# Causal mask and row maximum of a diagonal score tile in one VectorE instruction, in a planned transformer block

## The chip, the cores and the metric

The kernel runs on one core of one Trainium2 chip. The core has TensorE (PE, matmuls into PSUM banks; PEld are its weight loads), VectorE (DVE), ScalarE (ACT), GpSimd (POOL) and SyncE (SP, which issues most DMAs). Each engine works through its own instruction queue in order, and semaphores hold an instruction until what it needs is done. The metric is device time in microseconds of one execution. Before the change the median of three runs is 1046.6 us (1046.23 to 1047.99); the profiled execution took 1046.28 us, of which the span from the first to the last instruction is 1044.4 us.

## The reference

A macaron block over x of shape (4, 1024, 256), all in fp32: half a feed-forward layer, causal attention with 16 heads of 16 features, half a feed-forward layer again.

```python
x = x + 0.5 * ffn(layernorm(x))
x = x + attn(layernorm(x))
x = x + 0.5 * ffn(layernorm(x))

# attn: q, k with rotary embedding
att = einsum('bhqd,bhkd->bhqk', q, k) / sqrt(hd)
mask = triu(full((T, T), -inf), k=1)
att = softmax(att + mask, axis=-1)
out = einsum('bhqk,bhkd->bhqd', att, v)

# ffn: INTER = 704
hdn = silu((x @ gate_w.T) * gate_s) * ((x @ up_w.T) * up_s)
out = (hdn @ down_w.T) * down_s
```

## The kernel before

The 4096 rows are eight blocks of 512 tokens (two to a sequence of 1024). A block goes through feed-forward 1 (`ffn`), the projections (`qkv`), attention and feed-forward 2; several blocks are under way at once so that dense matmuls fill TensorE while attention waits for the vector engines. Matmuls come in two modes. Column matmuls (feed-forward, projections, probabilities times values) use four groups of 32 array columns side by side; row matmuls (scores) use four groups of 32 array rows, one head each. All dense products are recorded under L470, score matmuls under L859 (for the maxima) and L972 (for the exponentials), probabilities times values under L1019.

Attention makes the scores twice. `max_half` computes scores with queries on partitions for two heads of a group of four and takes the row maximum on VectorE; `row_of_max` turns the maxima (L939, a matmul with the identity), copies them to SBUF (L942) and sends them by DMA (L947) into a spare row of the queries, so that `exp_half`, which makes the scores again with keys on partitions, has the maximum subtracted by the matmul itself. ScalarE then takes the exponential from PSUM (L981), GpSimd zeroes what lies above the diagonal (L993), and `weigh` multiplies with the values. A max half and an exp half of different head pairs run at the same time as one burst on four row groups; each half owns two PSUM banks, one for each head `e` of its pair, until its last reader is done. One or two bursts in a row make a visit to row mode.

The units of `max_half` for one block and a pair of groups `gs`: off the diagonal (second block of a sequence only) whole tiles of 512 keys; on the diagonal, for each of the two groups, one of 512 and one split into 384 + 128, and one shared by both groups, 256 + 256. A unit's entry is (group, query tile, key block, first column, width, masked). On a diagonal entry the last 128 columns cross the diagonal. There, before the change, an addition of the 128x128 tile `causal` (zero and -1e30) masks these columns in PSUM (L884), and a reduction with `negate=True` takes the negative maximum into a column of the tile `nm` (L911, or L894 with one instruction for both groups of the shared unit). Where a sequence has two key blocks, L933 joins the two parts with a minimum.

Nothing of the order is left to a compiler's scheduler. The class `Planner` keeps a modelled time for each engine, with a duration and a priority for each `Op` (`dve_us(n)` is n/960 + 0.07), and places next whatever can start first, or a burst (`step`). PSUM has eight banks, shared between bursts ("score") and dense outputs ("d", at most four). A few thresholds (`GAP`, `LONG`, `SECOND`, `DUE`, `OPEN`) say how long bursts are held back; `draw` sets them anew after each eight bursts, from a table of seeds, which before the change is empty (all thresholds at their defaults). So a changed duration of one step moves instructions on all engines.

Of the kernel before, what the change touches and what calls it, by code (L numbers as in the profile page):

```python
# [13 lines left out]
F32 = mybir.dt.float32  # L14
AF = mybir.ActivationFunctionType
ALU = mybir.AluOpType
AX = mybir.AxisListType
PSUM = bass.MemoryType.PSUM

P = 128  # L20
EPS = 1e-5
MASKED = -1e30
DRAWS = ()


class Buf:
# [20 lines left out]
class Planner:  # L47
# [3 lines left out]
    ENGINES = ("pe", "dve", "act", "pool", "dma")  # L51
    GAP = 0.8
    LONG = 7.0
    VISIT = 2
    SECOND = 0.3
    OPEN = 3.0
# [111 lines left out]
    def step(self, burst):  # L168
        b = burst()

        more = self.mode == "row" and self.visit < self.VISIT and b is not None and {h.kind for h in b[1]} != {"max"}
        due = b is not None and (more or self.since >= self.GAP)
        best = None
        for eng in self.ENGINES:
            for c in self.candidates(eng):
                s = max(c[0], self.busy["pe"] + 0.05) if eng == "pe" else c[0]
                if eng == "pe" and due and any(k.slot is None and k.kind == "d" for k in c[2].takes):
                    s += self.DUE
                key = (s, c[1] + (self.luck[eng] * self.random() if self.luck[eng] else 0.0))
                if best is None or key < best[0]:  # L180
                    best = (key, c)
        if b is not None:
            pe = self.busy["pe"]
            at = max(b[0], pe)
            if more:
                wait = self.SECOND
            else:
                wait = self.WAIT[self.mode]
                if self.since < self.GAP:
                    at += self.GAP - self.since  # L190
                elif self.since < self.LONG and b[2] is not None:
                    at = max(at, b[2] - 0.853 - 0.2 - self.SECOND)
            key = (max(at, pe + 0.05) - wait, 0)
            if best is None or key < best[0]:
                halves = b[1]
                us = max(h.us for h in halves) + 0.02 + (0.0 if self.mode == "row" else self.CHANGE["row"])
                if self.mode == "row":

                    us += min(max(b[0] - pe + 0.2, 0.0), 0.1)
                at = max(b[0], pe, at if self.since >= self.GAP else 0.0)  # L200
                for h in halves:
                    h.us = us
                    self.place(h, at)
                self.visit = self.visit + 1 if self.mode == "row" else 1
                self.mode, self.since = "row", 0.0
                self.bursts += 1
                self.draw()
                return b
        assert best is not None, "nothing can be placed"
        (s, _), (at, _, op, q) = best  # L210
        if op.eng == "pe":
            self.since += op.us
            if op.mode != self.mode:
                op.us += self.CHANGE[op.mode]
                self.mode = op.mode
        self.place(op, at)
        for o in op.then:
            self.since += o.us
            self.place(o, self.busy["pe"])
        if q is not None:  # L220
            q.popleft()
        else:
            self.loose[op.eng].remove(op)
            self.unplaced -= 1
        return None
# [6 lines left out]
def dve_us(n):  # L232
    return n / 960 + 0.07
# [7 lines left out]
def tile_macaron(  # L241
# [16 lines left out]
    nc = tc.nc  # L258
# [51 lines left out]
    wo_sb = cpool.tile([P, NC, D], F32, name="wo_sb")  # L310
    rope_sb = cpool.tile([P, 2, T], F32, name="rope_sb")
    ident = cpool.tile([P, P], F32, name="ident")
    causal = cpool.tile([P, P], F32, name="causal")
    mhalf = cpool.tile([P, 2], F32, name="mhalf")
    lasting = dict(
        kT=[cpool.tile([P, NG, BLK], F32, name=f"kT_{i}", tag=f"kT_{i}") for i in range(3)],
# [28 lines left out]
    def consts():  # L345
        nc.scalar.dma_start(out=gus_sb, in_=gus)
        nc.scalar.dma_start(out=ds_sb, in_=ds.partition_broadcast(P))
        nc.scalar.dma_start(out=wd_sb[HALF:, NF, :], in_=wl)
        at = 0
        for a, e in cuts:  # L350
            part = wgu[at : at + D * (e - a)].rearrange("(p c i) -> p c i", p=P, c=NC)
            nc.sync.dma_start(out=wgu_sb[:, :, a:e], in_=part)
            at += D * (e - a)
        nc.sync.dma_start(out=wd_sb[:, :NF, :], in_=wd)
        nc.gpsimd.memset(mhalf, -0.5)
        make_identity(nc, ident)
        make_causal_mask(nc, causal, mask_val=MASKED)

    def scaled_gus():

# [483 lines left out]
    def row_at(g, part, h, j):  # L844

        return g % 2 * HP + part * GH * NB + h * NB + j

    def max_half(blk, unit, pair, nm, reduces):

        parts = 1 + blk % BPS  # L850
        sc = [Buf("score") for _ in range(2)]
        tiles = [kT[blk - parts + 1 + u[2]] for u in unit]

        def emit():

            for (g, j, _, c0, w, _), kt in reversed(list(zip(unit, tiles))):
                for e in range(2):
                    r = slice((2 * pair + e) * HP, (2 * pair + e) * HP + HD)
                    nc.tensor.matmul(  # L859
                        sc[e].tile[:, c0 : c0 + w],  # L860
                        qT[blk].tile[r, g, ts(j, P)],
                        kt.tile[r, g, :w],
                        start=True,
                        stop=True,
                    )

        gs = {u[0] // 2 for u in unit}
        need = [T_done[1, b, n] for b in range(blk - blk % BPS, blk + 1) for n in gs]
        first = Op(
            "pe", mm_us(sum(u[4] for u in unit)), emit, need, [*sc, nm], [qT[blk], *tiles], mode="row", tail=0.25  # L870
        )
        masked = [(c0 + w - P, c0 + w) for _, _, _, c0, w, m in unit if m]

        def head(e):
            prev = first
            if masked:

                def mask():
                    a, z = masked[0][0], masked[-1][1]
                    if masked[0][1] == masked[-1][0] or len(masked) == 1:  # L880
                        d = sc[e].tile[:, a:z].rearrange("p (m k) -> p m k", k=P)
                    else:
                        d = sc[e].tile.rearrange("p (m k) -> p m k", k=2 * P)[:, :, P:]
                    nc.vector.tensor_tensor(d, d, causal.unsqueeze(1).to_broadcast([P, len(masked), P]), ALU.add)  # L884

                prev = Op("dve", dve_us(P * len(masked)), mask, [first], uses=[sc[e]], prio=0, tail=0.1)
                loose_att.append(prev)

            if unit[0][0] != unit[-1][0]:
                j, part = unit[0][1:3]  # L890

                def reduce():
                    o = row_at(0, part, 2 * pair + e, j)
                    nc.vector.tensor_reduce(  # L894
                        nm.tile[:, o : o + HP + 1 : HP],
                        sc[e].tile.rearrange("p (g k) -> p g k", g=2),
                        AX.X,
                        ALU.max,
                        negate=True,
                    )  # L900

                o = Op("dve", dve_us(BLK), reduce, [prev, *filled["nm"]], uses=[sc[e], nm], prio=0, tail=0.25)
                loose_att.append(o)
                for g in (unit[0][0], unit[-1][0]):
                    reduces[g].append(o)
            else:
                for g, j, part, c0, w, _ in unit:

                    def reduce(g=g, j=j, part=part, c0=c0, w=w):
                        o = row_at(g, part, 2 * pair + e, j)  # L910
                        nc.vector.tensor_reduce(  # L911
                            nm.tile[:, o : o + 1], sc[e].tile[:, c0 : c0 + w], AX.X, ALU.max, negate=True
                        )

                    o = Op("dve", dve_us(w), reduce, [prev, *filled["nm"]], uses=[sc[e], nm], prio=0, tail=0.25)
                    loose_att.append(o)
                    reduces[g].append(o)

        for e in range(2):
            head(e)  # L920
        first.pair, first.kind = pair, "max"
        return first

    def row_of_max(blk, g, nm, reduces):
# [3 lines left out]
        if blk % BPS:  # L928

            def both():  # L930
                o = [row_at(g, n, 0, 0) for n in range(2)]
                a, b = (nm.tile[:, n : n + GH * NB] for n in o)
                nc.vector.tensor_tensor(a, a, b, ALU.min)  # L933

            need = [Op("dve", 0.09, both, reduces, uses=[nm], prio=0)]
            loose_att.extend(need)
# [2 lines left out]
            nc.tensor.matmul(d.tile[:HP, :P], nm.tile[:, ts(g % 2, HP)], ident, start=True, stop=True)  # L939

        def copy():
            nc.scalar.copy(t.tile, d.tile[: GH * NB, :P])  # L942

        def send(pair):
            for h in (2 * pair, 2 * pair + 1):
# [359 lines left out]
```

## Time and profile before

| | before |
|---|---|
| median of 3 runs | 1046.6 us |
| profiled execution | 1046.28 us |
| its span | 1044.4 us |
| granted TensorE clock | 1.000 |
| VectorE busy at L884 (masks), 320 instructions | 103.9 us |
| VectorE busy at L911 (reduces), 640 instructions | 330.3 us |
| VectorE busy at L894 (reduces for two groups), 64 instructions | 40.8 us |
| VectorE busy in all | 808.5 us |

Busy time counts an engine's instructions that move or compute data, overlapping ones once. The means in the groups are those of single instructions and hold the overlap with the next. The page's digit rows divide the span into 40 slices and give tenths; PEclk is at 9 (90% or more) in all of them. The chain of waits follows the work back from the last instruction, at each step to what released it. Matmul ends are modelled, so that PE is shown busy also where it loses time between matmuls; its starts are measured.

### The profile page before, as it was taken

Reading aid. Unit: us, or ns where it says so; the run is one execution under the profiler, and the core shown is the slowest. Engines: PE = TensorE matmul, PEld = TensorE weight load, DVE = VectorE, ACT = ScalarE, POOL = GpSimd, SP = SyncE. Lnnn points to the kernel's source line nnn. Section 1 sums busy time; section 2 is a strip of 40 time slices with the busy share of each in tenths; the row PEclk is TensorE's granted clock in tenths of the full one; section 3 lists DMA queues with packets and bytes.
Section 4 is the critical chain, followed back from the end, with each engine's and each line's share of the span. In section 5 each row is a group of like instructions: output and inputs, shape, how many; then the busy total and the mean of one; then the engine's idle time right before and its main releaser. Section 6 shows DMA issues by size and latency. Waiting matters only on the chain.

```text
span 1044.4 us, 28697 instructions
## 1 busy us (share of the span) xinstructions
PE 1036.3 (99%) x12162; PEld 442.7 (42%) x12162; DVE 808.5 (77%) x1876; ACT 429.7 (41%) x821; POOL 295.1 (28%) x501
## 2 busy tenths in 40 slices
PE   9999999999999999999999999999999999999998
PEld 5434443343444444443434443342434443434443
DVE  6679889788898887888897798778896797884432
ACT  3314341444453452435454434544354444455411
POOL 5222542231121633312115424221226211112200
PEclk9999999999999999999999999999999999999999
DMA  7211202102020021111010103101012010010000
GB/s 290 62 42 38 66 3 62 42 2 62 22 42 23 12 61 34 37 48 22 32 52 8 37 2 72 32 13 52 3 38 50 22 39 22 12 52 3 21 22 22
DMA packets 37969, 41.10 MB, mean 39 GB/s; under 512 B 3985, under 2 KB 27729, under 8 KB 37713
## 3 DMA queue, kind: packets, MB, share of 16 engines
q1 hardware_dynamic: 37184, 38.81, 14.1%
q8 instruction: 95, 1.56, 0.6%
q10 hardware_dynamic: 656, 0.47, 0.2%
q14 instruction: 34, 0.27, 0.1%
HBM read 19.60 MB, written 15.20 MB: 33 GB/s over the span
## 4 chain that ended last, share of the span: by engine, by line
PE 92%; DVE 6%; DMA 1%; issue 0%; ACT 0%; SPq 0%; DVEq 0%
PE bank L470 54%; PE bank L859 17%; PE bank L1019 12%; PE bank L972 10%; DVE nm L911 1%; DVE bank L884 1%; DVE xs L491 1%; DVE nm L894 1%; PE bank L939 0%; DVE hT L626 0%; DVE ta L623 0%; DMA xd<-xs 0%; PE bank L520 0%; DVE ta L603 0%; DVE hL L606 0%
## 5 line engine op out<-in xcount | busy, mean ns | idle before, releaser
L981 ACT ACTIVATE pT<-bank 128x512 f32<-128x512 f32 x576 | 298.5, 603 | 307.5 <-PE bank L972 306.7
L911 DVE TENSOR_REDUCE nm<-bank 128x1 f32<-128x512 f32 (+2 forms) x640 | 330.3, 573 | 20.0 <-PE bank L972 17.8
L470 PE MATMUL bank<-xnT,wgu_sb 128*32 128x512 f32 (+1 forms) x2832 | 321.5, 592 | 0.3
L859 PE MATMUL bank<-kT,qT 16*128 16x512 f32 (+3 forms) x1536 | 286.8, 511 | 2.2 <-DVE x L1104 0.9
L972 PE MATMUL bank<-qT,kT 17*128 17x512 f32 (+3 forms) x1536 | 286.7, 514 | 0.0
L470 PEld LDWEIGHTS bank<-xnT,wgu_sb 128*32 128x32 f32 x2832 | 92.0, 109 | 194.6 <-issue 122.1
L993 POOL TENSOR_SCALAR_AFFINE_SELECT pT<-pT 128x256 f32<-128x256 f32 x256 | 99.1, 407 | 263.9 <-ACT pT L981 263.0
L859 PEld LDWEIGHTS bank<-kT,qT 16*128 16x128 f32 x1536 | 111.3, 184 | 141.7 <-issue 35.3
L470 PE MATMUL bank<-wd_sb,hT 128*32 128x256 f32 x2560 | 152.4, 379 | 0.0
L1019 PE MATMUL bank<-pT,va 128*32 128x512 f32 (+3 forms) x1536 | 137.5, 487 | 0.4 <-DVE nm L911 0.2
L884 DVE TENSOR_TENSOR bank<-bank,causal 128x256 f32<-128x256 f32 (+1 forms) x320 | 103.9, 370 | 20.3 <-PE bank L972 15.1
L972 PEld LDWEIGHTS bank<-qT,kT 17*128 17x128 f32 x1536 | 109.4, 184 | 9.4 <-issue 2.6
L470 PEld LDWEIGHTS bank<-wd_sb,hT 128*32 128x32 f32 x2560 | 85.4, 110 | 55.1 <-issue 2.6
L620 ACT ACTIVATE ta<-bank,gus_sb 128x512 f32<-128x512 f32 x80 | 55.0, 687 | 113.2 <-PE bank L470 100.8
L623 DVE SCALAR_TENSOR_TENSOR ta<-ta,bank 128x512 f32<-128x512 f32 x80 | 54.6, 683 | 44.4 <-ACT ta L620 43.6
L1019 PEld LDWEIGHTS bank<-pT,va 128*32 128x32 f32 x1536 | 51.7, 109 | 83.5 <-issue 59.9
L1058 POOL TENSOR_TENSOR oq<-oq 128x512 f32<-128x512 f32 x32 | 40.7, 1273 | 154.8 <-DVE oq L1055 151.9
L1055 DVE STREAM_TRANSPOSE oq<-bank 128x512 f32<-128x512 f32 x64 | 45.5, 711 | 35.1 <-PE bank L1019 34.5
L626 DVE SCALAR_TENSOR_TENSOR hT<-bank,gus_sb,ta 128x512 f32<-128x512 f32 x80 | 59.5, 744 | 16.7 <-PE bank L470 15.5
L652 DVE TENSOR_TENSOR x<-bank,x 128x256 f32<-128x256 f32 x64 | 26.8, 418 | 49.7 <-PE bank L470 49.3
L731 POOL TENSOR_TENSOR qs<-qs,rope_sb 128x512 f32<-128x512 f32 x32 | 40.8, 1277 | 79.7 <-DVE qs L728 60.0
L470 PE MATMUL bank<-xnT,wqkv_sb 128*32 128x512 f32 x512 | 60.6, 595 | 0.1
(61 smaller groups left out, 649.0 us busy)
## 6 DMA issues: line engine op xcount, KB each, us to landing
xd<-xs SPq DMA_DIRECT2D x84, 128.0 KB
xnT<-xd SPq DMA_DIRECT2D x21, 512.0 KB
kT<-qT SPq DMA_DIRECT2D x64, 64.0 KB
x<-in_x SPq DMA_DIRECT2D x7, 512.0 KB
out<-x SPq DMA_DIRECT2D x14, 256.0 KB
qT<-nmT SPq DMA_DIRECT2D x128, 2.0 KB
wgu_sb<-in_wgu SPq DMA_DIRECT2D x2, 512.0 KB
rope_sb<-in_rope SPq DMA_DIRECT2D x1, 1024.0 KB
```

Of the source, the lines that this page charges most:

```text
L470: nc.tensor.matmul(out[ts(m, HP)], w[:, ts(m, HP)], x, **kw)
L620: nc.scalar.activation(a.tile, d.tile, AF.Tanh, scale=gus_sb[:, 0, c : c + 1])
L623: nc.vector.scalar_tensor_tensor(a.tile, a.tile, 1.0, d.tile, ALU.add, ALU.mult)
L626: nc.vector.scalar_tensor_tensor(hT[c].tile, e.tile, gus_sb[:, 1, c : c + 1], a.tile, ALU.mult, ALU.mult)
L859: nc.tensor.matmul(sc[e].tile[:, c0 : c0 + w], qT[blk].tile[r, g, ts(j, P)], kt.tile[r, g, :w], start=True, stop=True,)
L884: nc.vector.tensor_tensor(d, d, causal.unsqueeze(1).to_broadcast([P, len(masked), P]), ALU.add)
L911: nc.vector.tensor_reduce(nm.tile[:, o : o + 1], sc[e].tile[:, c0 : c0 + w], AX.X, ALU.max, negate=True)
L972: nc.tensor.matmul(sc[e].tile[:, c0 : c0 + w], kt.tile[r, g, ts(k % NB, P)], qT[blk].tile[r, g, BLK - w :], start=True, stop=True,)
L981: nc.scalar.activation(pT.tile[:, e, :w], sc[e].tile[:, :w], AF.Exp)
L993: nc.gpsimd.affine_select(out=d, in_=d, compare_op=ALU.is_ge, fill=0.0, base=0, pattern=[[0, 2], [1, P]], channel_multiplier=-1,)
L1019: nc.tensor.matmul(av.tile[ts(r, HP), BLK - w :], va[base + k // NB].tile[:, k % NB, h * VS : h * VS + HP], pTs[u, r // 2].tile[:, r % 2, ...
L1055: nc.vector.transpose(o.tile, av.tile)
```

## The change

Masking and reducing a diagonal entry become one VectorE operation, `tensor_tensor_reduce`: it adds `causal` to the scores, writes the sum back to the bank, and keeps the running maximum, which goes to the column of `nm`. As it runs over the entry's whole width, `causal` grows to 128x512, zero in the first 384 columns, and each entry uses its last `w` columns. The shared unit gets two such operations in place of one reduction for both groups. The operation can't negate its maximum, so maxima stay positive until L942, where the copy becomes a multiplication by -1, and L933 takes a maximum. In the planner, a fused step has the duration `dve_us(w)`. A new rule (`SLACK`) holds a step of lower priority back on VectorE and ScalarE when an urgent one becomes ready while it would run, unless it would end within 0.3 us (VectorE) or 0.1 us (ScalarE) of that. The table `DRAWS` gets 36 seeds, one for each eight bursts: 0 means the defaults, a negative seed moves each threshold by up to 3%, a positive one draws them from wide ranges and adds a random part to priorities.

```diff
-DRAWS = ()
+DRAWS = (
+    0, 607770, -440924, -671785, 0, 0, 0, 0, 518923, 731658, 0, 0, 0, 342111, -717196, -551854,
+    520586, 932614, 0, 0, -22380, 0, 556666, 0, 883259, 627517, 102005, 0, -129261, -32818, 0,
+    0, -79134, 466540, -412283, 867698,
+)
...
+    SLACK = dict(dve=0.3, act=0.1)
...
-            for c in self.candidates(eng):
+            found = list(self.candidates(eng))
+            first = min((c[0] for c in found if c[1] == 0), default=None) if eng in ("dve", "act") else None
+            for c in found:
                 s = max(c[0], self.busy["pe"] + 0.05) if eng == "pe" else c[0]
...
+                if first is not None and c[1] and s < first < s + c[2].us - self.SLACK[eng]:
+
+                    s = first + 0.001
...
-    causal = cpool.tile([P, P], F32, name="causal")
+    causal = cpool.tile([P, BLK], F32, name="causal")
...
-        make_causal_mask(nc, causal, mask_val=MASKED)
+        nc.gpsimd.memset(causal[:, : BLK - P], 0.0)
+        make_causal_mask(nc, causal[:, BLK - P :], mask_val=MASKED)
...
-                    nc.vector.tensor_tensor(d, d, causal.unsqueeze(1).to_broadcast([P, len(masked), P]), ALU.add)
-
-                prev = Op("dve", dve_us(P * len(masked)), mask, [first], uses=[sc[e]], prio=0, tail=0.1)
-                loose_att.append(prev)
-
-            if unit[0][0] != unit[-1][0]:
+            if unit[0][0] != unit[-1][0] and not any(u[5] for u in unit):
...
+            for g, j, part, c0, w, m in unit:
+
+                def reduce(g=g, j=j, part=part, c0=c0, w=w, m=m):
+                    o = row_at(g, part, 2 * pair + e, j)
+                    a, n = sc[e].tile[:, c0 : c0 + w], nm.tile[:, o : o + 1]
+                    if m:
+
+                        nc.vector.tensor_tensor_reduce(a, a, causal[:, BLK - w :], 1.0, MASKED, ALU.add, ALU.max, n)
+                    else:
+                        nc.vector.tensor_reduce(n, a, AX.X, ALU.max)
+
+                o = Op("dve", dve_us(w), reduce, [first, *filled["nm"]], uses=[sc[e], nm], prio=0, tail=0.25)
+                loose_att.append(o)
+                reduces[g].append(o)
...
-                nc.vector.tensor_tensor(a, a, b, ALU.min)
+                nc.vector.tensor_tensor(a, a, b, ALU.max)
...
-            nc.scalar.copy(t.tile, d.tile[: GH * NB, :P])
+            nc.scalar.mul(t.tile, d.tile[: GH * NB, :P], -1.0)
```

## The prediction

> **What bounds the kernel now.** I read the page first (busy time and the chain of waits), then a table by stretches of the span, then groups by form for VectorE's prices, and last the timeline around two attention bursts.
>
> ```profile
> span 1044.4 us, 28697 instructions
> PE 1036.3 (99%) x12162; PEld 442.7 (42%) x12162; DVE 808.5 (77%) x1876; ACT 429.7 (41%) x821; POOL 295.1 (28%) x501
> ...
> DVE  6679889788898887888897798778896797884432
> ...
> PE 92%; DVE 6%; DMA 1%; issue 0%; ACT 0%; SPq 0%; DVEq 0%
> ```
>
> ```profile
> 60.00:950.00 890.00, 887.13 (x10336) 374.42 (x10332) 740.81 (x1719) 386.77 (x744) 255.82 (x438) 1.00 0.14 34
> ```
>
> The columns of the second fence are the stretch, its length, then PE, PEld, DVE, ACT, POOL busy and the granted clock (1.00). The reader is to see two things: TensorE fills the span, and VectorE, which the change relieves, fills 740.8/890 = 83% of the stretch in which attention runs. A busy PE is not a PE at its peak, so I cut the PE timeline wherever row matmuls (scores, L859 and L972) and column matmuls (the rest) change places, and compare each piece with its columns.
>
> ```profile
> 417.56 0.42 PE bank L972 x2
> 417.98 0.01 PE bank L859 x2
> 417.99 1.91 PE bank L470 x32
> 419.89 0.63 PE bank L859 x2
> ...
> 421.83 1.86 PE bank L470 x32
> ```
>
> These are pieces of the chain: start, length, work. Four matmuls of 512 columns run side by side in 0.853 us where nothing interrupts (weight loads of a long L470 stretch come in fours every 0.43 us, two passes each), which is 2,400 columns per us over all four. The column piece at 417.99 holds two such groups, 1.71 us, and takes 1.91; the row visit at 419.89 holds two bursts, again 1.71, and takes 1.94.
>
> Over the whole trace: 2,265,088 columns / 2,400 = 943.8 us of work that no order can shorten. On top, 160 column pieces each lose at least 0.16 us (median 0.17: 26.4 us in all), 133 two-burst visits lose 0.25 to 0.36 us by shape and 22 one-burst visits 0.22 (together some 45 us). This is the price of changing mode. What is left over these floors is only **15 us of real stalls**, 5 in row visits and 10 in column pieces; in most of the largest (0.9 us at 170, 0.6 at 783, 0.6 at 235) the row's first weight load waited for a VectorE operation (L1104, L626, L1055). About 14 us lie at the two ends and in the transposes. So a VectorE saving can win at most 15 us, whatever its size.
>
> **The change, part by part.** *Mask and reduce become one step.* Prices before:
>
> ```profile
> L911 DVE TENSOR_REDUCE nm<-bank 128x1 f32<-128x512 f32 x384 | 240.5, 680 | 20.0 <-PE bank L972 17.8 <-PE bank L859 1.7
> L884 DVE TENSOR_TENSOR bank<-bank,causal 128x256 f32<-128x256 f32 x192 | 72.5, 423 | 11.5 <-PE bank L972 9.6 <-ACT va L769 1.5 <-PE bank L859 0.3
> ...
> L623 DVE SCALAR_TENSOR_TENSOR ta<-ta,bank 128x512 f32<-128x512 f32 x80 | 54.6, 683 | 44.4 <-ACT ta L620 43.6
> ...
> L933 DVE TENSOR_TENSOR nm<-nm 128x16 f32<-128x16 f32 x16 | 2.6, 163 | 0.0
> ...
> L728 DVE LOAD_MASK_SELECT qs<-bank x32 | 0.4, 13 | 12.3 <-PE bank L470 8.4 <-POOL qT L734 3.1 <-POOL on L1074 0.7
> ```
>
> The columns after the bar are busy us and mean ns of one. A mean contains the overlap with the next, so I take the step from start to start:
>
> ```profile
> 430.17 0.49 DVE L884 TENSOR_TENSOR bank<-bank,causal 128x128 f32<-128x128 f32 x2
> 430.56 1.27 DVE L911 TENSOR_REDUCE nm<-bank 128x1 f32<-128x512 f32 x2
> ...
> 434.12 0.76 DVE L884 TENSOR_TENSOR bank<-bank,causal 128x256 f32<-128x256 f32 x2 [0.31 <-PE bank L972]
> 434.80 1.41 DVE L911 TENSOR_REDUCE nm<-bank 128x1 f32<-128x384 f32 x4
> ```
>
> Two 128-wide masks 0.39, so 0.198 each; two 256-wide 0.68, so 0.33 each; reduces step by 0.598 (512), 0.465 (384) and 0.198 (128). Mask and reduce follow one line, width/960 us + 0.065. For each block, pair of groups, pair and head of the pair (8 x 2 x 2 x 2 = 64 times) there are two diagonal 512 units, two 384+128 units, and one 256+256 unit. Before: 2 x (0.198 + 0.598) + 2 x (0.331 + 0.465 + 0.198) + (0.331 + 0.598) = 4.51 us, times 64 = 288.6 us. The built order of the changed kernel has 512 fused steps and, behind each, a second VectorE instruction that writes one column of nm. At the same line the fused steps take 2 x 0.598 + 2 x (0.465 + 0.198) + 2 x 0.331 = 3.18 us, times 64 = 203.8 us, plus 512 r, where **r** is what the second instruction adds. Even at r = 0.166 us.
>
> The second instruction is what the Trainium skill announces (VectorE: DVE Perf Modes, "Two Vector instructions with no wait between them": an operation that also writes its accumulator is a main one and an accumulator read). Counting diff lines alone would give 84.8 us saved; counting by this rule it is 84.8 - 512 r. No row shows r. Its floor is LOAD_MASK_SELECT, which moves no tensor (13 ns); its ceiling the small L933, which starts only when the reduce before it has drained and is followed by the next after 0.19. I take 0.10, between them: an instruction without input, yet behind a drain. Saved: 84.8 - 51.2 = 33.6 us, between 78 and -12. In the middle VectorE falls from 740.8 to 707 of 890 us, 79%.
>
> The rule against this change stands in the skill's Vector Engine (DVE) Microarchitecture Reference, "Points that are easy to get wrong": the tensor-tensor shape with two non-bf16 SBUF sources runs at half rate, since both read ports are taken and none is left for the accumulator. At half rate the fused steps would need 163,840/960 = 170.7 us more, and VectorE 740.8 - 33.6 + 170.7 = 878 of 890 us. Here one source is PSUM, and the L623 row has that mix (SBUF ta, PSUM bank) at 683 ns for 512, near the reduce's 680: one element per cycle. It has no accumulator, so I keep half rate as a small rival and take full rate.
>
> *Negation* moves into L942's copy, an ACT operation on 16x128 in both kernels (245 ns): nothing. *max for min* at L933: nothing. *The wider causal tile* adds a GpSimd memset of 384 columns at the start, about 0.4 us from the 128-column one (204 ns) and the 2048-column one (1,797 ns). GpSimd has been idle from 1.9 to 5.3 us there, waiting for the first statistics, so it is hidden; without cover it would cost its 0.4.
>
> *The order.* The shorter steps, the hold-back of low-priority work on VectorE and ScalarE and the 36-entry table make another order on every engine. Same columns, but the built order has 161 row visits instead of 155: 127 of two bursts and 34 of one. At the floors: 6 more column pieces x 0.17 = 1.0 us, rows +0.7: **+1.7 us**, certain, as it is counted.
>
> *The stalls.* VectorE is shorter in the bursts, and the hold-back keeps short-deadline work at the head of its in-order queue: what waits behind a large low-priority step (a transpose, L626) is what stalls now. Against it, the planner books width/960 + 0.07 for a fused step and nothing for the read: each diagonal half gives up its two banks 2r to 4r later than planned, with ScalarE's work and the next visit behind. With a mean 6 us from visit to visit and 17% of VectorE idle, that is 1 us of slack against 0.2 to 0.4 late, so mostly absorbed. I take just under half of the 15 us as won: -7. Sum on the profiled execution (span 1044.4, total 1046.28): 1046.3 + 1.7 - 7 = **1041 us**. The median of the runs, 1046.6, is 0.3 above, below what I can resolve.
>
> **Rivals.**
> 1. *Nearly all stalls go* (VectorE was their only cause, r small): 1046.3 + 1.7 - 13 = 1035. For it: VectorE names in most large stalls. Against: some waits were chosen, a visit put off so as to hold two bursts. Chance 0.13.
> 2. *TensorE-bound, nothing to win*: stalls move rather than vanish, the extra visits eat the rest: 1046, within 2 us. For it: 99% and 15 us in all. Chance 0.15.
> 3. *The unbooked accumulator read makes VectorE late (slower).* Place: the bank release after diagonal halves, 160 of 288 max halves. From r = 0.166 VectorE does more than before while the order expects 85 us less. At r = 0.25, 512 x 0.25 - 84.8 = +43 us, 88% of the middle; a fifth of the added 43 passed on to TensorE is 9, with 1.7 for the visits 1057; at r = 0.19 about 1050. Chance 0.15.
> 4. *Half rate*: 878 of 890 us; at the 93% or so of its fullest slices VectorE needs 944 us for the stretch: about 1100. Chance 0.04.
>
> The forecast itself (1037 to 1043.5) has 0.53. A measurement of this kernel tells from no change about 0.2%, 2.1 us. Faster: 0.53 + 0.13 and a little of 2, so 0.66; same 0.15; slower 0.19. The range, 1034 to 1052, takes in rivals 1 and 2 and the mild end of 3 and leaves out some 0.15. The side below no change has most of the chance, with 1034 to 1044 as its own range.
>
> **What would show it.** Fused rows near 0.68 us for 512 and a read row: a step from one fused start to the next of 0.70 confirms r = 0.1; 0.77 or more is rival 3, 1.1 rival 4. VectorE busy near 775 us. PE pieces: floors as before and stalls near 8 us. I am wrong if PE loses to something other than VectorE, such as ScalarE's exponentials or the nmT transfers moved in the queue, or if the changed order costs more per visit.

## The result, and the profile after

The changed kernel takes **1061.89 us** (median of 4 runs, 1061.49 to 1062.26) against 1046.48 us before (median of 4): a ratio of **1.0143**, 95% interval 1.0129 to 1.0158. It is slower, by 15.4 us, where 5 us of gain were forecast. The profiled span is 1060.6 us, 16.2 more than before.

The page after, with the rows that answer to those shown of before:

```profile
span 1060.6 us, 28981 instructions
PE 1041.8 (98%) x12162; PEld 444.3 (42%) x12162; DVE 772.7 (73%) x2132; ACT 431.1 (41%) x821; POOL 296.6 (28%) x502
...
DVE  6678779888777787876668697687895877684432
...
PE 82%; DVE 15%; issue 1%; DMA 1%; ACT 0%; POOL 0%; SPq 0%; DVEq 0%
```

VectorE is busy 35.8 us less (808.5 to 772.7), and yet the chain of waits runs through it for 15% of the span where it was 6%. The engine that was relieved is waited for more. The groups by form give the price of a fused step, whose name in the trace is CUSTOM_DVE_ANT_0 (busy us, mean ns of one, then idle time before it):

```profile
L911 DVE TENSOR_REDUCE nm<-bank 128x1 f32<-128x512 f32 x256 | 159.3, 682 | 19.8 <-PE bank L970 19.3 <-PE bank L870 0.2
L909 DVE CUSTOM_DVE_ANT_0 bank<-bank,causal 128x512 f32<-128x512 f32 x128 | 85.1, 720 | 13.7 <-PE bank L970 10.9 <-PE bank L870 2.6
L909 DVE CUSTOM_DVE_ANT_0 bank<-bank,causal 128x384 f32<-128x384 f32 x128 | 74.3, 587 | 8.8 <-PE bank L970 8.2 <-PE bank L870 0.3
L909 DVE DVE_READ_ACCUMULATOR2_ANT nm<- 128x1 f32 x512 | 72.2, 141 | 0.0
```

The 128 columns between 384 and 512 cost 133 ns more, 960 elements per us in each partition, as with the reduce; behind each fused step stands a read of the accumulator of 141 ns. What a read takes of the queue depends on what follows, and the timeline shows it together with the stall it makes. These are VectorE and TensorE in a visit with two max halves of 384 + 128, its first step and its end (start us, length us, engine and line, what was done, in brackets the idle time before it):

```profile
227.04 0.57 DVE L909 CUSTOM_DVE_ANT_0 bank<-bank,causal 128x384 f32<-128x384 f32 x1
...
229.73 0.60 DVE L909 CUSTOM_DVE_ANT_0 bank<-bank,causal 128x384 f32<-128x384 f32 x1
230.25 0.14 DVE L909 DVE_READ_ACCUMULATOR2_ANT nm<- 128x1 f32 x1
230.42 0.30 DVE L909 CUSTOM_DVE_ANT_0 bank<-bank,causal 128x128 f32<-128x128 f32 x1
230.64 0.14 DVE L909 DVE_READ_ACCUMULATOR2_ANT nm<- 128x1 f32 x1
230.64 0.71 DVE L1053 STREAM_TRANSPOSE oq<-bank 128x512 f32<-128x512 f32 x1
230.83 0.19 PEld L870 LDWEIGHTS bank<-kT,qT 16*128 16x128 f32 x2 [1.46 <-DVE nm L909]
230.84 0.48 PE L870 MATMUL bank<-kT,qT 16*128 16x256 f32 x2 [0.55 <-DVE nm L909]
```

From the 384-wide step to the 128-wide one in the same bank it is 0.69 us, where width/960 + 0.065 gives 0.465: the second step of a bank starts 0.03 us after the first one's read has ended (230.39), and that read costs 0.22. The read behind the 128-wide step overlaps with the transpose that follows and costs some 0.02. The two halves of this visit, eight fused steps, run from 227.04 to 230.64, **3.60 us; the planner booked 4 x (0.470 + 0.203) = 2.69**. The next burst waits for the last of them, and TensorE stands 0.55 us. Mask and reduce, before, took 4.00 us for two such halves, from 434.12 to 438.12, and were booked at 4 x 0.337 + 2.69 = 4.04, so about right (lines of before; the next operation starts at 438.12):

```profile
434.12 0.76 DVE L884 TENSOR_TENSOR bank<-bank,causal 128x256 f32<-128x256 f32 x2 [0.31 <-PE bank L972]
434.80 1.41 DVE L911 TENSOR_REDUCE nm<-bank 128x1 f32<-128x384 f32 x4
436.12 0.76 DVE L884 TENSOR_TENSOR bank<-bank,causal 128x256 f32<-128x256 f32 x2
436.78 1.40 DVE L911 TENSOR_REDUCE nm<-bank 128x1 f32<-128x384 f32 x4
438.12 0.01 DVE L728 LOAD_MASK_SELECT qs<-bank  x1
```

Measured as in the prediction, TensorE's real stalls are 28.1 us instead of 14.7 (+13.4); the floors of 161 visits make 73.7 instead of 71.7 (+2.0); the first dense matmul comes at 9.50 instead of 8.75 (+0.75, in this one profile; not pursued). Together 16.2 us, the whole difference of the spans.

### The profile page after: what moved, and what is told of

Read it like the earlier page. It is cut to its first block, busy times and chain, and to the rows that moved or that the text cites. A ratio compares the mean times of both kernels' runs of the same rounds, so it can differ in the third digit from the quotient of the medians.

```text
span 1060.6 us, 28981 instructions
## 1 busy us (share of the span) xinstructions
PE 1041.8 (98%) x12162; PEld 444.3 (42%) x12162; DVE 772.7 (73%) x2132; ACT 431.1 (41%) x821; POOL 296.6 (28%) x502
## 4 chain that ended last, share of the span: by engine, by line
PE 82%; DVE 15%; issue 1%; DMA 1%; ACT 0%; POOL 0%; SPq 0%; DVEq 0%
PE bank L481 48%; PE bank L870 14%; PE bank L1017 10%; DVE bank L909 9%; PE bank L970 8%; DVE nm L909 2%; DVE xs L502 1%; DMA wgu_sb<-in_wgu 1%; DVE st L428 1%; PE bank L937 1%; DVE hT L637 1%; DVE x L663 0%; DVE oq L1053 0%; DVE ta L634 0%; DVE hL L617 0%
## 5 line engine op out<-in xcount | busy, mean ns | idle before, releaser
L481 PE MATMUL bank<-xnT,wgu_sb 128*32 128x512 f32 (+1 forms) x2832 | 325.3, 593 | 2.0 <-DVE ta L634 0.9
L909 DVE CUSTOM_DVE_ANT_0 bank<-bank,causal 128x128 f32<-128x128 f32 (+3 forms) x512 | 242.2, 515 | 33.9 <-PE bank L970 24.4
L481 PEld LDWEIGHTS bank<-xnT,wgu_sb 128*32 128x32 f32 x2832 | 96.5, 109 | 187.7 <-issue 114.9
L911 DVE TENSOR_REDUCE nm<-bank 128x1 f32<-128x512 f32 x256 | 159.3, 682 | 19.8 <-PE bank L970 19.3
L991 POOL TENSOR_SCALAR_AFFINE_SELECT pT<-pT 128x256 f32<-128x256 f32 x256 | 99.8, 409 | 251.6 <-ACT pT L979 250.9
L481 PE MATMUL bank<-wd_sb,hT 128*32 128x256 f32 x2560 | 154.7, 379 | 0.0
L909 DVE DVE_READ_ACCUMULATOR2_ANT nm<- 128x1 f32 x512 | 72.2, 141 | 0.0
```

Source lines behind the costliest of these rows:

```text
L481: nc.tensor.matmul(out[ts(m, HP)], w[:, ts(m, HP)], x, **kw)
L909: nc.vector.tensor_tensor_reduce(a, a, causal[:, BLK - w :], 1.0, MASKED, ALU.add, ALU.max, n)
L911: nc.vector.tensor_reduce(n, a, AX.X, ALU.max)
L991: nc.gpsimd.affine_select(out=d, in_=d, compare_op=ALU.is_ge, fill=0.0, base=0, pattern=[[0, 2], [1, P]], channel_multiplier=-1,)
```

## The experiments

Theory R: the order is made for a VectorE that is faster than the real one, and what runs later than its booking stalls TensorE. Rivals: F, the fused step itself holds TensorE up; O or N, the new order is bad whatever VectorE takes; T and H, the table or the hold-back is at fault. The runs in one table, each with its ratio to the kernel before on the same chip, its 95% interval, VectorE's busy time and TensorE's stalls (of them those after 900 us) in its profile. What TensorE loses while its granted clock is down counts among the stalls; from the mean clock this is some 20 us in run 2 (0.982) and 12 in run 8 (0.989), an estimate, and under 8 in each of the others:

| run | median us | ratio | DVE busy us | stalls us (late) |
|---|---|---|---|---|
| before | 1046.5 to 1046.9 | | 808.5 | 14.7 (1.5) |
| changed kernel | 1061.89 | 1.0143 [1.0129, 1.0158] | 772.7 | 28.1 (2.3) |
| 1 fused, old order | 1043.22 | 0.9967 [0.9956, 0.9979] | 772.8 | 11.3 (1.5) |
| 2 two steps, new order | 1134.20 | 1.0848 [1.0811, 1.0885] | 849.5 | 100.1 (11.5) |
| 3 entries apart, new order | 1049.40 | 1.0026 [1.0016, 1.0036] | 757.0 | 16.3 (1.6) |
| 4 no mask, new order | 1042.93 | 0.9963 [0.9950, 0.9976] | 734.7 | 9.9 (1.2) |
| 5 no table | 1082.32 | 1.0342 [1.0315, 1.0368] | 775.9 | 48.4 (9.7) |
| 6 no table, no hold-back | 1079.62 | 1.0313 [1.0297, 1.0328] | 774.6 | 45.4 (7.8) |
| 7 as 6, read booked | 1058.25 | 1.0104 [1.0089, 1.0119] | 775.7 | 26.9 (13.1) |
| 8 as 6, booked twice | 1064.34 | 1.0164 [1.0149, 1.0179] | 773.6 | 34.5 (1.6) |
| 9 as 5, read booked | 1060.56 | 1.0114 [1.0087, 1.0141] | 776.3 | 28.6 (15.1) |
| 10 changed kernel, read booked | 1049.36 | 1.0020 [1.0012, 1.0027] | 773.6 | 15.6 (1.1) |
| 11 as 10, own table | 1044.02 | 0.9970 [0.9960, 0.9979] | 774.6 | 12.2 (1.2) |
| 12 as 11, entries apart | 1043.09 | 0.9965 [0.9952, 0.9978] | 758.5 | 10.3 (1.2) |
| 13 before, own table | 1044.98 | 0.9985 [0.9977, 0.9993] | 810.2 | 12.2 (1.1) |
| 14 fused, old order, apart | 1041.51 | 0.9949 [0.9934, 0.9964] | 754.2 | 10.0 (1.5) |
| 15 no mask, old order | 1041.30 | 0.9954 [0.9939, 0.9969] | 726.7 | 10.1 (1.5) |
| 16 no mask, own plan and table | 1040.98 | 0.9946 [0.9930, 0.9963] | 732.0 | 9.5 (1.0) |

### The instruction alone, and the order alone (runs 1 and 2)

In run 1 the planner of before makes the order, with mask and reduce as two steps of its model; where the mask was placed nothing is issued, where a reduce of a diagonal entry was placed the fused step is.

```diff
                 def mask():
-                    nc.vector.tensor_tensor(d, d, causal..., ALU.add)
+                    pass
...
+                        if m:
+                            nc.vector.tensor_tensor_reduce(a, a, causal[:, BLK - w :], 1.0, MASKED, ALU.add, ALU.max, n)
```

> The fused step alone: every engine's order is that of the kernel before; where a mask stood nothing is issued, where a reduce of a masked entry stood the fused step is. If the new order is what costs (theory O), VectorE has some 36 us less to do in an unchanged order and the time falls below 1046.5: 1036 to 1045. If the fused step itself holds TensorE up (theory F: the bank or the maximum comes late behind its accumulator read), the time rises here too: 1055 or more.

1043.22 us: faster than before, and theory F falls. VectorE's busy time (772.8) is that of the changed kernel; only the order differs, and 18.7 us lie between the two.

Run 2 is the reverse: the changed kernel's order with mask and reduce as two instructions.

```diff
-                        nc.vector.tensor_tensor_reduce(a, a, causal[:, BLK - w :], 1.0, MASKED, ALU.add, ALU.max, n)
+                        if c0 == 0:
+                            nc.vector.tensor_tensor(d, d, k, ALU.add)
...
+                    nc.vector.tensor_reduce(n, a, AX.X, ALU.max)
```

> The order of the changed kernel, but mask and reduce as two instructions as before (a mask over two entries of a unit in one), so VectorE has about 40 us more than in the changed kernel and each diagonal unit ends 0.1 to 0.35 us later than there. Theory O (the order costs, VectorE has room): within 6 us of the changed kernel's 1062, 1058 to 1068. Theory R (the order is tight on VectorE and what runs later than its booking stalls TensorE): clearly slower, 1068 to 1085. Theory F: faster than the changed kernel, near 1048.

1134 us, far beyond what even theory R expected. Its page:

```profile
span 1131.7 us, 28772 instructions
PE 1069.9 (95%) x12162; PEld 448.2 (40%) x12162; DVE 849.5 (75%) x1940; ACT 432.2 (38%) x821; POOL 295.6 (26%) x502
...
PE 68%; DVE 28%; issue 2%; ACT 1%; DMA 0%; POOL 0%; SPq 0%; DVEq 0%; ACTq 0%
```

A VectorE that is busy only 75% of the span costs TensorE 100 us. Some 20 of them are the lower clock. Occupancy says little here; what counts is whether a step is done when the order expects it.

### The same order with a faster VectorE (runs 3 and 4)

Both leave the order of TensorE, ScalarE, GpSimd and SyncE as it is in the changed kernel. In run 3 the two fused steps of a bank no longer follow each other: the first entries of both heads come first.

```diff
+        turn = [(e, *u) for u in unit for e in range(2)]
...
+                    e, g, j, part, c0, w, m = turn.pop(0)
```

> The changed kernel with its order on all engines but VectorE, where the two fused steps of one bank no longer follow each other, which takes about 18 us off VectorE (773 to 755) by shorter waits on the read. Theory R (the order is only late): the stalls fall by some 7 to 12 us, the time to 1049 to 1056. Theory N (the order is bad in itself): within 3 us of 1062.

In run 4 the mask before the maximum is left out, so that a step takes what was booked.

```diff
-                        nc.vector.tensor_tensor_reduce(a, a, causal[:, BLK - w :], 1.0, MASKED, ALU.add, ALU.max, n)
+                        nc.vector.tensor_reduce(n, a, AX.X, ALU.max)
```

> The changed kernel's order on all engines, but the diagonal entries are only reduced, without the mask, so each takes on VectorE what the planner booked (width/960 + 0.07). The mask before the maximum is left out; the one after the exponential stays. Theory R: stalls back to 8 to 15 us, time 1038 to 1047. Theory N: 1055 or more.

With run 2 and the changed kernel this makes a row in one order: VectorE busy 734.7, 757.0, 772.7, 849.5 us; time 1042.9, 1049.4, 1061.9, 1134.2 us; stalls 9.9, 16.3, 28.1, 100.1 us. From the first to the last, 115 us on VectorE cost 91 us of time; from run 4 to the changed kernel, 38.0 us more of busy VectorE come with 18.2 us more of stalls, nearly half. Theory N falls: where steps take what was booked, the changed order is 3.6 us faster than the kernel before, in spite of its 161 visits. The page of run 4:

```profile
span 1041.5 us, 28420 instructions
...
PE 96%; DVE 2%; ACT 1%; issue 0%; DMA 0%; POOL 0%; SPq 0%; DVEq 0%; ACTq 0%
```

The chain's share on VectorE falls from 15% to 2%.

### Table and hold-back (runs 5 and 6)

```diff
-DRAWS = (0, 607770, ...)
+DRAWS = ()
...
-                if first is not None and c[1] and s < first < s + c[2].us - self.SLACK[eng]:
-                    s = first + 0.001
```

Run 5 has the first edit, run 6 both.

> The changed kernel without its table of 36 seeds: all thresholds at their defaults, the hold-back of low-priority steps kept. If the table is at fault (theory T) the time returns to 1040 to 1047. If any order planned with the short booking of the fused step is late (theory R), it stays at 1055 to 1068.

> The changed kernel without table and without hold-back: the planner's rules of before, only the fused step and its booking of width/960 + 0.07 are new. Theory T or H (table or hold-back at fault): 1040 to 1047. Theory R (short booking): 1055 to 1068, like the changed kernel. 162 row visits against 155 explain about 2 us either way.

The table isn't at fault: without it the time is 20 us longer still. The upper ends expected were passed as well, so something besides R is at work in these two; the next runs show a part of it. With the hold-back the time is 2.7 us longer here, but the intervals overlap, as they do in the booked pair below (runs 7 and 9).

### Booking the read (runs 7 to 10)

```diff
-                o = Op("dve", dve_us(w), reduce, ...)
+                us = dve_us(w) + (0.0 if not m else 0.05 if w == BLK else 0.1)
+                o = Op("dve", us, reduce, ...)
```

Run 8 books 0.2 us for each fused step.

> No table, no hold-back, and the planner books the accumulator read with the fused step: 0.05 us more for a 512-wide step, 0.10 for each of two steps in one bank (measured: 0.05; 0.19 and 0.02). Theory R (the order is made for a VectorE that is faster than the real one): TensorE's stalls fall from 45 us to below 16 and the time from 1079.6 to 1036 to 1046. Theory N (any order other than the one of before is worse, the booking is not the cause): still 1060 or more.

> As the booked kernel, but 0.2 us more for each fused step, twice what they take: the planner believes VectorE some 60 us slower than it is. Theory R: no stalls from late steps, but some time given up by caution: 1036 to 1048. Theory N: 1060 or more.

> The booked kernel with the hold-back of low-priority steps. Theory R: 1036 to 1046, within 4 us of the booked kernel. Theory H (the hold-back idles VectorE and ScalarE and costs time of its own): 5 us or more above the booked kernel.

> The changed kernel with nothing but the booking of the read added: hold-back and table stay. The table's seeds were made for another order, so here they are any seeds. Theory R: 1038 to 1050, at least 12 below the changed kernel's 1062. Theory T (the table is at fault): 1055 or more.

In the changed kernel itself (run 10) the booking alone takes 12.5 us off, and the stalls go from 28.1 to 15.6, as before the change. Without a table (run 7 against 6) it takes off 21 us, but 1058 misses what theory R expected. Up to 900 us the stalls are right, 13.8 us where run 6 has 37.7 and before has 13.2. The rest, 13.1 us, lies at the end. Run 7, then run 10, in the stretch from 980 to 1020 us (length, then PE, PEld, DVE, ACT, POOL busy, granted clock):

```profile
980.00:1020.00 40.00, 32.98 (x399) 16.16 (x393) 9.64 (x23) 14.72 (x29) 9.87 (x18) 0.87 0.02 8
```

```profile
980.00:1020.00 40.00, 40.00 (x508) 16.69 (x504) 18.21 (x38) 8.69 (x16) 4.89 (x10) 1.00 0.06 22
```

In run 7 the last row visit is at 1001.7 us, in run 10 at 977.2: there attention ends while no dense work is left to lie beside it, TensorE waits for exponentials, and its granted clock falls to 0.87. With the read booked, what the table does is to bring attention to its end in time. Run 9, without it, has 15.1 us of late stalls, much as run 7; it lies within 4 us of run 7, as expected, and like run 7 misses the range of time that was expected of it. Run 8 misses too, and its 1064 is what theory N expected, though N fell with run 4. It has no such end, but 18.9 us of stalls between 300 and 400 us, most of them from 329 to 361, where the granted clock is 0.63 to 0.69; why its order stalls there I did not pursue. Booking too much is no cure.

### Orders made for right bookings (runs 11 to 13)

Run 11 books 0.05 us for a 512-wide step, 0.20 and 0.02 for the first and second of a bank, and has a table of seeds chosen on the planner's own clock for these bookings. Run 12 adds the steps of a unit entry by entry instead of head by head, books 0.05 for each, and has its own table. Run 13 is the kernel before with nothing but a table.

```diff
+                us = dve_us(w) + (0.0 if not m else 0.05 if w == BLK else 0.02 if c0 else 0.2)
```

> The changed kernel with the read booked as measured (0.05 for a 512-wide step, 0.20 and 0.02 for the two steps of one bank) and with a table of seeds chosen for this booking. Theory R: 1036 to 1043, stalls at or below the kernel before, faster than the fused step in the old order. If a table chosen on the planner's clock brings nothing on the chip: 1046 or more.

> As the previous one, with the two steps of one bank kept apart (all heads' first entries, then the second), each read booked at 0.05, and a table chosen for that. Theory R: 1034 to 1042. If keeping them apart only lets the planner pack VectorE more tightly than it is, 1046 or more.

> The kernel before, mask and reduce as two instructions, with a table of seeds chosen for it and nothing else. If tables are worth something by themselves: 1038 to 1045. If the order of before was as good as its bookings allow: 1045 to 1050.

Runs 11 and 12 (1044.0, 1043.1) end 1 us above what theory R expected, at stalls of 10 to 12 us; still 18 to 19 us below the changed kernel. Run 11 is not faster than the fused step in the old order (run 1, 1043.2), as theory R had it. A table alone, on the old instructions, brings some 1.5 us (ratio 0.9985).

### What the step can bring at most (runs 14 to 16)

Run 14 is run 1 with the first entry's fused step issued where the mask was placed, the second's where the reduce was, so that no two steps of a bank follow each other. Runs 15 and 16 leave the mask before the maximum out, in the old order and in an order of their own with a table.

```diff
                 def mask():
-                    pass
+                    fused(*unit[0][:5])
```

> The order of the kernel before with fused steps, but the two steps of one bank no longer follow each other: the first entries of both heads come first, then the second entries. If the 0.19 us of an accumulator read comes from the next step's wait on the same bank, VectorE's busy time falls from 773 us to 745 to 760; TensorE has only 11 us of stalls left in this order, so the time stays within 3 us of 1043: 1040 to 1044.

> The order of the kernel before, with no mask before the maximum (left out; the one after the exponential stays): about 100 us less on VectorE than before. TensorE has 15 us of stalls to win in this order, and the fused step won 4 to 5 of them: 1039 to 1043.

> No mask before the maximum (left out; the one after the exponential stays), one reduction for the shared unit, the hold-back, and a table chosen for this plan; bookings are right without any addition. If right bookings and a table are what an order needs: 1036 to 1042. If the floor of stalls is near 10 us in any order: 1041 to 1045.

Run 14's timeline on VectorE, at two halves of 384 + 128 (columns as above):

```profile
67.70 0.57 DVE L882 CUSTOM_DVE_ANT_0 bank<-bank,causal 128x384 f32<-128x384 f32 x1 [0.28 <-PE bank L860]
68.18 0.14 DVE L882 DVE_READ_ACCUMULATOR2_ANT nm<- 128x1 f32 x1
68.18 0.60 DVE L882 CUSTOM_DVE_ANT_0 bank<-bank,causal 128x384 f32<-128x384 f32 x1
...
68.70 0.33 DVE L882 CUSTOM_DVE_ANT_0 bank<-bank,causal 128x128 f32<-128x128 f32 x1
...
70.72 0.68 DVE L624 SCALAR_TENSOR_TENSOR ta<-ta,bank 128x512 f32<-128x512 f32 x1
```

The next step now starts together with the read, 0.48 to 0.52 us after a 384-wide one instead of 0.66 to 0.69, and the two halves take 3.02 us (67.70 to 70.72) instead of 3.60. Run 14 beats both kernels at 1041.51 us and leaves nothing out. To leave the mask out altogether, 22 to 28 us less on VectorE, brings hardly more (1041.3, 1041.0): at some 10 us of stalls, VectorE is hardly what TensorE still waits for (2% of the chain of waits in runs 14 and 15, 1% in run 16). That mask isn't needed for the softmax, which is the same for any subtracted bound as long as the exponentials don't vanish, since L991 (L993 before the change) zeroes what lies above the diagonal; whether that holds for other inputs was not tried.

## Why the prediction was wrong

- **VectorE's saving: right.** Forecast 33.6 us at r = 0.10, measured 35.8. Behind the sum, r is 0.05 or less where the next step is independent and about 0.2 where it is in the same bank; the mean is (84.8 - 35.8)/512 = 0.096. That the assumed 0.10 met this mean is luck: no step has it, the two sorts were not told apart, and the second, 0.22 in the visit shown, lies above the ceiling of 0.19 that was taken from L933.
- **Full rate: right.** The fused steps run at 960 elements per us, so rival 4 falls. The rule cited there from the Trainium skill (Vector Engine (DVE) Microarchitecture Reference, "Points that are easy to get wrong") is stated for the scalar-tensor-tensor shape with both sources in SBUF; no run here tests it, since one source of the fused step lies in PSUM.
- **Negation, GpSimd's memset: right** as far as seen; no stall of those listed goes back to either.
- **At most 15 us to win: held, and too high as an estimate.** Six runs with a lighter VectorE and right or generous bookings (1, 4, 12, 14, 15, 16) end at 9.5 to 11.3 us of stalls, run 11 at 12.2, so no run gave back more than some 5 of the 14.7 us; even with right bookings -7 was 2 us too much.
- **The price of the visits: right.** +1.7 forecast, +2.0 measured.
- **The stalls: wrong, and this is the step that failed**: "With a mean 6 us from visit to visit and 17% of VectorE idle, that is 1 us of slack against 0.2 to 0.4 late, so mostly absorbed. I take just under half of the 15 us as won: -7." They grew by 13.4. The lateness of one half was about right, 0.45 us measured; but 134 of the 161 visits hold two max halves, so it adds up to 0.9 in the one shown. The slack was wrong. VectorE is idle for 27% of the new span, but the planner places each step as soon as its model allows, and TensorE stood 0.55 us behind that visit. Over the whole order nearly half passed on (18.2 us of stalls for 38.0 us of busy VectorE, run 4 against the changed kernel), where the forecast had most of it absorbed.
- **Rival 3 named the mechanism and its place, with the wrong point.** It was to decide "from r = 0.166", where VectorE has more to do than before. What decides is the difference between a step and its booking, whatever was there before: a mean r of 0.096 was enough. Its sign, 0.77 us or more from one 512-wide start to the next, did not come either: 0.65 was measured. In the same order, the row from 735 to 849.5 us of VectorE shows it without a change of load on any other engine.
- **Table and hold-back** had no sign of their own in the forecast. The table gains 20 us in this plan, 7 of them in stalls after 900 us, while the cause of the rest stays open; with the read booked (run 9 to 10) it gains 11, all of them there. For the hold-back no gain was found.

## What to carry to other kernels

Where an order is planned from booked durations, a cheaper instruction changes two things: the work, and the truth of the bookings. Measure the new step from start to start in the sequence in which it will stand, with its hidden second instruction and its waits, and book that before anything else is judged; test the instruction first in the old order. And idle time of an engine is no slack for a plan that has been made again: the slack is in the difference between booking and duration.

## What the runs showed of the hardware

The accumulator read is a row of 141 ns that starts 83 ns before the fused step's own row ends. A next step in another bank starts with it, and the pair takes 0.05 us more than a reduce of that width (0.648 against 0.598 us at 512); one in the same bank starts when the read is done, about 0.2 us later than a reduce's successor would.

TensorE's granted clock can fall after a short idle time. In run 7 a gap of 2.25 us before the matmul at 985.80 goes with a clock of 0.50 from 984.8 to 991.6, and one of 2.27 us before 1005.11 with 0.50 from 1005.3 to 1008.7 (first the matmul, then the stretches, with columns as in the pair of stretches above; the ends of matmuls are modelled, so the gaps are too):

```profile
985.80 4.49 PE L1011 MATMUL bank<-pT,va 128*32 128x512 f32 x32 [2.25 <-ACT pT L973]
```

```profile
984.80:991.60 6.80, 5.80 (x40) 2.43 (x44) 0.72 (x1) 1.83 (x4) 1.08 (x3) 0.50 0.01 2
...
1005.30:1008.70 3.40, 3.40 (x28) 1.51 (x24) 0.00 (x0) 0.00 (x0) 0.49 (x2) 0.50 0.00 0
```

The length of a gap alone does not decide. Gaps of 1.35 us (before 994.25) and 1.16 us (before 999.82) leave the clock at 1.00 in run 7, but in run 9 gaps of these lengths (before 992.88 and 1000.14) go with 0.50 from 993.2 to 996.6 and from 1000.0 to 1003.4, and in run 2, where no gap is over 1.65 us, the clock is at 0.50 eleven times before 900 us. So a stall can be paid for twice; over all of run 2 the clock is 0.982.
